# A two-layer block with a selective scan: later accumulating transfers, a later silu and router, spreads first, more convolution on TensorE

## The chip, the cores and the metric

One Trainium2 chip, of which the program uses one core. The metric is the device time of one execution in microseconds, the median of three runs.

## The reference

Two layers over `x` of 4 x 256 tokens with 512 features, all in float32. Only the second layer is touched by the change.

```python
xn = layernorm(x)
x = x + attention(xn) + ffn(xn)                 # layer 0
xn = layernorm(x)
x = x + ssm(xn) + moe(xn)                       # layer 1

def ssm(h):                                     # DIN = 1024, N = 16, K = 4
    x, z = split(h @ in_proj_w)                 # 512 -> 2 x 1024, then as b d l
    xc = silu(conv_b + sum(conv_w[:, k] * pad(x)[:, :, k:k + L] for k in range(4)))
    p = xc @ x_proj_w.T                         # 32 + 16 + 16 columns
    dt_r, Bm, Cm = rmsnorm of each part
    dt = softplus(dt_r @ dt_proj_w.T + dt_bias)
    h_t = exp(dt_t * A) * h_{t-1} + dt_t * B_t * xc_t        # 1024 x 16 states
    y_t = sum over n of h_t * C_t
    return ((y + D * xc) * silu(z)) @ out_proj_w.T

def moe(x):
    base = x @ base_W.T
    w = softmax(x @ router_W.T), top 2 of 8, normalised, 0 elsewhere
    mid = (x @ lora_A) * w                      # 8 experts x rank 16
    return base + 2 * (mid @ lora_B)
```

## The kernel before

The program is written by hand in order: every engine runs its instructions in the order in which the Python code emits them, and semaphores between the engines follow from the data. SyncE (SP) issues the plain transfers, GpSimd (POOL) the accumulating ones. VectorE is DVE, ScalarE ACT and TensorE PE.

Layer 0 and the preparation of batch 0 take the first 325 us. What the change touches is the scan phase after that. The four batches b are scanned one after the other, each as 32 units: eight chunks c of 128 channels times four groups g of four states (`PER` = 32 units in a batch, `NU` = 4 in a chunk). A unit holds 128 partitions (4 states x 32 channels) by 4 x 256 columns. Its steps are:

- `decays(u)`, ACT: four exponentials of 255 columns into one of four `decay` buffers, emitted three units ahead;
- `scan_in(u)`, DVE: `bx = B * (dt * xc)` (line 995). Before it stands a wait for the landed `du` of the chunk, the unit's decays, and the state sums of unit u-4, whose buffer `h` it is about to reuse;
- `scan(u)`: the scan on DVE (line 1009), then `h * C` on POOL (line 1014);
- `states_sum(u-1)`, PE: four matmuls that add the states into `ysum` (line 1026), with `D * xc` (line 1024) at a chunk's first unit. There is one `ysum`, so this first matmul waits until `take_sum` has copied the last chunk's sum to SBUF (ACT, line 1031);
- `gate`, POOL: `y * silu(z)` (line 1034).

`dt` and `dt * xc` come out as 128 channels by 256 columns; `send` stores a pair of chunks to memory (line 939) and `spread` reads one chunk back as 32 x 4 lines, in four transfers (line 944), into one of two buffers.

While a batch is scanned, the next one is prepared, and the outputs of earlier ones are finished. The pieces are hung on units by hand: `put(b, s, f, ...)` places a call ahead of the scan of unit s of batch b, `put_mid` between `scan_in` and `scan`, `put_late` after the scan and `put_end` after the sum. Within a unit, the copy of a finished sum (`take_sum`) and the decays come first. The pieces are:

- `norm_*`, then `px_mm` (line 763), the projection of a pair p of chunks of the next batch, two matmul groups in units 6 to 13;
- `conv_in` and `conv_taps`: the convolution over four taps. The first chunk of a pair goes over PE with diagonal weights (`dg`, made by ACT, line 810) from batch 1 on. The second one does so too for the pairs in `both`; else ACT makes three scaled copies (`tap`, line 791) and POOL adds them up (line 817);
- `conv_out`, `conv_silu` (ACT, line 826, with `gate_silu`, line 959, and a table load before and after), then `pp_mm`, `pp_square` and `pp_norm` (DVE, line 851);
- `step_in` and `step_exp` (ACT), `step_out` (POOL, lines 920, 922 and 924) and `step_x` (POOL, line 931): the next `dt` and `dt * xc`, with a `send` at the last of each;
- `pz_mm` and `gate_silu` for `silu(z)`;
- `router`, `route` (15 small DVE steps, lines 1061 to 1093), `expert_mid`, `expert_turn`, `expert_out`: the experts of two batches at a time;
- `dense` and `out_mm`: the base and the output projection, row block by row block. For batches 0 to 2 the scanned layer's output is not added on chip: `store_x` first writes the residual to the output, and `add_out` copies a PSUM group over `x` (ACT) and adds it to the output by an accumulating transfer (POOL). One such group holds `dense` and `expert_out`, the other `out_mm`.

PSUM has three general buffers (`psmm`), which all the groups above share.

Of the kernel before, what the change touches and what calls it, by code (L numbers as in the profile page):

```python
# [26 lines left out]
DC = DIN // P  # L27
# [14 lines left out]
def block_kernel(  # L42
# [25 lines left out]
    mm = nc.tensor.matmul  # L68
# [50 lines left out]
    live = {}  # L119
# [416 lines left out]
    first, second = latents(0), latents(1)  # L536
# [62 lines left out]
    first, second = latents(2), latents(3)  # L599
# [166 lines left out]

    both = ((1, 0), (1, 3), (2, 1), (2, 3), (3, 1), (3, 3))

# [345 lines left out]

    def dense(b, i, k):
        if k == 0:
            live["po", b, i] = psmm.tile([P, D], F32, tag="mm", name="po1")
        for hc in (2 * k, 2 * k + 1):
            mm(live["po", b, i], lhsT=xns[b][:, hc, i * P : (i + 1) * P], rhs=late_w["bw"][:, hc, :],
               start=(hc == 0), stop=False)  # L1120

    stored = {}

    def rows_of(tb):
        return out_d[tb * P : (tb + 1) * P, :]
# [3 lines left out]

    def add_out(tb, po):  # L1130

        nc.scalar.copy(x[:, tb, :], po)  # L1132
        d = nc.gpsimd.dma_start(rows_of(tb), x[:, tb, :], accum_op=ALU.add)
        tc.add_manual_dep(d.ins, stored[tb].ins.name, early, reason="sums in place")
        stored[tb] = d

    def expert_out(b, i):
        po, last = live["po", b, i], b == B - 1
        if last:
            mm(po, lhsT=ident, rhs=x[:, 2 * b + i, :], start=False, stop=False)  # L1140
        mm(po, lhsT=live["mt"][:, i * P : (i + 1) * P], rhs=late_w["lb"], start=False, stop=not last)
        if not last:
            add_out(2 * b + i, live.pop(("po", b, i)))

    def out_mm(b, i, c):
        if c == 0 and b < B - 1:
            live["po", b, i] = psmm.tile([P, D], F32, tag="mm", name="po2")
        mm(live["po", b, i], lhsT=xcs[b][:, c, i * P : (i + 1) * P], rhs=late_w["ow"][:, c, :],  # L1148
           start=(c == 0 and b < B - 1), stop=(c == DC - 1))
        if c == DC - 1 and b < B - 1:  # L1150
            add_out(2 * b + i, live.pop(("po", b, i)))

# [121 lines left out]

    at, mid_at, late_at, end_at = {}, {}, {}, {}
# [12 lines left out]
    def put_late(b, s, f, *a):  # L1288

        late_at.setdefault(b * PER + s, []).append((f, a))  # L1290

    for b in range(B):
        nxt = b + 1
        if b:
            put(b, 0, b_rows, b, 1)
            put(b, 0, spread, "du", b, 1)

            put(b, 0, gate_silu, b, 0, 1)
            for k, u in enumerate((0, 1, 1, 2)):
                put(b, u, dense, b - 1, k // 2, k % 2)  # L1300
            put(b, 2, expert_turn, b - 1)
            for i in range(2):
                put(b, 3, expert_out, b - 1, i)

            for (bo_, i), us in {
                1: {(0, 0): range(22, 30)},
# [3 lines left out]
            }[b].items():  # L1310
                for c, u in enumerate(us):
                    put(b, u, out_mm, bo_, i, c)
        else:
# [44 lines left out]
        if nxt < B:  # L1358
# [11 lines left out]
            for p in range(NP):  # L1370
                put(b, 2 * p if b else (5, 6, 9, 9)[p], load_x, nxt, p)
# [10 lines left out]
            put_late(b, 21, step_in, nxt, 0, 0)  # L1382
            put(b, 22, step_in, nxt, 0, 1)
            put(b, 22, c_rows, nxt, 0)
            put(b, 23, step_exp, nxt, 0, slice(0, 2))
            put(b, 23, step_exp, nxt, 0, slice(2, 4))
            put(b, 23, c_rows, nxt, 1)
            for q, us in enumerate(((24, 25, 26), (28, 30, 32))):
                for k in range(3):
                    put(b, us[k], step_out, nxt, 0, q, k)  # L1390
            put(b, 27, step_x, nxt, 0)
            put(b, 27, spread, "dt", nxt, 0)
            put(b, 29, spread, "du", nxt, 0)
            put(b, 33, step_x, nxt, 1)
            put(b, 30, b_rows, nxt, 0)
            put(b, 31, spread, "dt", nxt, 1)
            put(b, 23, load_z, nxt, 0)
# [3 lines left out]
            if b % 2 == 0:  # L1401
                for i, u in enumerate((16, 17, 19, 20)):
                    put(b, u, router, b, i)
                choice = route()
                for w, u in ((0, 22), (0, 23), (0, 24), (1, 25), (0, 25), (0, 26), (1, 27), (0, 27),
                             (0, 28), (1, 29), (0, 29), (1, 30), (0, 30), (0, 31), (0, 32)):
                    (put_mid if w else put_late)(b, u, next, choice)
                for i in range(2):
                    put_late(b, 32 + i, expert_mid, b, i)
# [15 lines left out]
    for u in range(total + 2):  # L1425
# [153 lines left out]
```

## Time and profile before

| | us |
|---|---|
| median of three runs | 832.85 (832.42 to 832.89) |
| the profiled execution | 835.05 |
| its span, first to last instruction | 833.0 |
| first `bx` of the scan phase | 325.5 |
| batch 0, 1, 2, 3 of the scan | 135.5, 122.9, 123.3, 125.8 |
| busy over the span: PE, DVE, ACT, POOL | 735.7, 652.1, 557.2, 509.0 |
| mean granted clock of TensorE | 0.953 |

The span is shorter than the execution's time; the rest lies around the first and the last instruction. A row of the timeline gives the start, the busy time, the engine, the line and the operation with output and inputs; in brackets at its end stand the idle time of the engine before it and what ended that. A wait for several semaphores is put down to the one that the profile shows as the last, which can be a neighbour of the right one where two end close together. The records of POOL are rough, above all for some units after a transfer was issued there, where neighbouring operations seem to overlap.

### The profile page before, as it was taken

Reading aid. Unit: us, or ns where it says so; the run is one execution under the profiler, and the core shown is the slowest. Engines: PE = TensorE matmul, PEld = TensorE weight load, DVE = VectorE, ACT = ScalarE, POOL = GpSimd, SP = SyncE. Lnnn points to the kernel's source line nnn. Section 1 sums busy time; section 2 is a strip of 40 time slices with the busy share of each in tenths; the row PEclk is TensorE's granted clock in tenths of the full one; section 3 lists DMA queues with packets and bytes.
Section 4 is the critical chain, followed back from the end, with each engine's and each line's share of the span. In section 5 each row is a group of like instructions: output and inputs, shape, how many; then the busy total and the mean of one; then the engine's idle time right before and its main releaser. Section 6 shows DMA issues by size and latency. Waiting matters only on the chain.

```text
span 833.0 us, 11255 instructions
## 1 busy us (share of the span) xinstructions
PE 735.7 (88%) x3834; PEld 428.6 (51%) x3834; DVE 652.1 (78%) x590; ACT 557.2 (67%) x1132; POOL 509.0 (61%) x406
## 2 busy tenths in 40 slices
PE   4999999999999999989887869788889878899985
PEld 2665545666555676656544346444346544334331
DVE  4586755287734435898699999899998899998996
ACT  4335574435556277599897798788898796865660
POOL 3223322001333333677969799969699978899875
PEclk9899999999999999979998979899999998999998
DMA  7234232001223332566395645534655534547500
GB/s 227 64 102 122 82 102 63 1 1 39 77 76 82 113 57 64 151 170 174 95 243 157 167 99 139 126 102 114 177 115 126 127 102 102 118 95 169 125 26 25
DMA packets 70371, 89.86 MB, mean 108 GB/s; under 512 B 12413, under 2 KB 52361, under 8 KB 70186
## 3 DMA queue, kind: packets, MB, share of 16 engines
q1 hardware_dynamic: 58794, 65.81, 29.8%
q0 software_dynamic: 10800, 21.50, 10.7%
q10 hardware_dynamic: 720, 1.84, 0.7%
q8 instruction: 30, 0.49, 0.3%
q14 instruction: 27, 0.22, 0.1%
HBM read 66.58 MB, written 13.37 MB: 96 GB/s over the span
## 4 chain that ended last, share of the span: by engine, by line
PE 49%; DVE 16%; POOL 11%; ACT 9%; issue 7%; DMA 7%; SPq 1%; POOLq 0%; ACTq 0%; DVEq 0%
PE pg L444 7%; POOL h L1014 6%; DVE h L1009 6%; PE pu L444 5%; DVE bx L995 4%; DMA dus<-dud 4%; PE px L763 4%; PE av L397 4%; PE po L469 3%; PE ysum L1026 3%; PE px L810 3%; PE pz L953 3%; PE scT L386 2%; DVE mpl L354 2%; ACT decay L983 2%
## 5 line engine op out<-in xcount | busy, mean ns | idle before, releaser
L1014 POOL TENSOR_TENSOR h<-h,cr 128x1024 f32<-128x1024 f32 (+1 forms) x130 | 312.8, 2432 | 50.6 <-DVE h L1009 41.2
L1009 DVE TENSOR_TENSOR_SCAN h<-decay,bx 128x1024 f32<-128x1024 f32 (+1 forms) x129 | 288.1, 2236 | 6.5 <-PE po L469 1.9
L983 ACT ACTIVATE decay<-dts,aneg 128x255 f32<-128x255 f32 x504 | 212.1, 501 | 35.9 <-DVE h L1009 17.7
L995 DVE TENSOR_TENSOR bx<-brow,dus 128x1024 f32<-128x1024 f32 x128 | 157.6, 1231 | 27.6 <-PE ysum L1026 10.9
L1026 PE MATMUL ysum<-h,stack 128*32 128x256 f32 x1024 | 87.6, 417 | 35.8 <-POOL h L1014 35.5
L456 POOL TENSOR_TENSOR hlo<-g,hhi 128x512 fp32r<-128x512 f32 x28 | 35.8, 1280 | 114.0 <-ACT hhi L455 114.0
L354 DVE TENSOR_REDUCE mpl<-sc 128x4 f32<-128x1024 f32 x64 | 76.7, 1220 | 22.2 <-PE sc L352 20.8
L427 POOL DMA_DIRECT2D wgu<-in_wgu x56 | 31.0, 554 | 94.6 <-PE pg L444 93.6
L388 ACT ACTIVATE pe<-scT 128x1024 f32<-128x1024 f32 x64 | 64.0, 1023 | 22.9 <-PE sc L352 14.2
L1026 PEld LDWEIGHTS ysum<-h,stack 128*32 128x32 f32 x1024 | 21.8, 112 | 90.1 <-POOL h L1014 61.6
L1148 PE MATMUL po<-ow,xc 128*128 128x512 f32 x128 | 65.4, 634 | 2.9 <-ACT x L1132 2.5
L953 PE MATMUL pz<-xn1T,w_in 128*128 128x256 f32 x256 | 65.0, 400 | 0.0
L763 PE MATMUL px<-xn1T,w_in 128*128 128x256 f32 x256 | 63.5, 395 | 0.4 <-ACT sz L959 0.3
L953 PEld LDWEIGHTS pz<-xn1T,w_in 128*128 128x128 f32 x256 | 48.8, 197 | 18.9 <-issue 11.2
L763 PEld LDWEIGHTS px<-xn1T,w_in 128*128 128x128 f32 x256 | 49.2, 197 | 14.2 <-issue 4.9
L452 DVE SCALAR_TENSOR_TENSOR g<-g,pg 128x512 f32<-128x512 f32 x28 | 19.2, 687 | 43.0 <-ACT g L451 43.0
L444 PE MATMUL pg<-xhi,wgu 128*128 128x512 f32 x112 | 49.6, 443 | 1.4 <-ACT xhi L244 1.4
L469 PE MATMUL po<-wd,hhi 128*128 128x512 f32 x112 | 49.4, 441 | 0.0
L444 PE MATMUL pu<-xhi,wgu 128*128 128x512 f32 x112 | 47.4, 423 | 0.8 <-DVE g L454 0.8
L455 ACT CAST hhi<-g 128x512 fp32r<-128x512 f32 x28 | 17.3, 620 | 45.8 <-DVE g L454 45.8
L444 PE MATMUL pg<-xlo,wgu 128*128 128x512 f32 x112 | 45.3, 404 | 0.7 <-DVE xlo L251 0.7
L444 PE MATMUL pu<-xlo,wgu 128*128 128x512 f32 x112 | 44.3, 396 | 0.0
(239 smaller groups left out, 1296.8 us busy)
## 6 DMA issues: line engine op xcount, KB each, us to landing
dts<-dtd SPq DMA_DIRECT2D x124, 128.0 KB, 3.1
dus<-dud SPq DMA_DIRECT2D x124, 128.0 KB, 3.3
wgu<-in_wgu POOLq DMA_DIRECT2D x56, 256.0 KB, 2.8
w_in<-in_inz SPq DMA_DIRECT2D x16, 512.0 KB, 5.3
w_in<-in_inx SPq DMA_DIRECT2D x14, 512.0 KB, 5.3
dtd<-dt SPq DMA_DIRECT2D x15, 256.0 KB, 2.2
dud<-du SPq DMA_DIRECT2D x15, 256.0 KB, 2.2
wd<-in_wd POOLq DMA_DIRECT2D x7, 512.0 KB, 3.6
```

What stands on the lines that cost most here:

```text
L354: nc.vector.tensor_reduce(mpl2[b % 2][:, qb, 2 * hp : 2 * hp + 2, 16 + 2 * gq : 18 + 2 * gq], sc.rearrange("p i (f k) -> p i f k", f=2), A ...
L388: nc.scalar.activation(pes[b, k][:, 2 * t : 2 * t + 2, :], sc, AF.Exp)
L444: mm(ps, lhsT=wgus[i][:, hc, :], rhs=xs[j][:, hc, :], start=(hc == 0 and j == 0), stop=(hc == HC - 1 and j == 1))
L469: mm(po, lhsT=hids[th][j][:, m, i * P : (i + 1) * P], rhs=wd[:, m, :], start=False, stop=(m == MC - 1 and j == 1))
L763: mm(px[:, i, :], lhsT=w[:, i, hc, :], rhs=xns[b][:, hc, :], start=(hc == 0), stop=(hc == HC - 1))
L953: mm(pz[:, i, :], lhsT=w[:, i, hc, :], rhs=xns[b][:, hc, :], start=(hc == 0), stop=(hc == HC - 1))
L983: made["da", u] = nc.scalar.activation(da[:, k, 1:], live["dts", b, c][:, k, 1:], AF.Exp, scale=aneg[:, c, k, g : g + 1])
L995: nc.vector.tensor_tensor(bx, brow[g // 2][:, g % 2, :].unsqueeze(1).to_broadcast([P, NG, S]), live["dus", b, c], ALU.mult)
L1009: nc.vector.tensor_tensor_scan(h[:, n].rearrange("p n t -> p (n t)"), da[:, n].rearrange("p n t -> p (n t)"), bx[:, n].rearrange("p n t -> ...
L1014: made["hc", u] = (nc.vector if k == NG - 1 else nc.gpsimd).tensor_tensor(h[:, n], h[:, n], crows[b][:, g, :].unsqueeze(1).to_broadcast([P ...
L1026: made["sum", u] = mm(ysum[k * NB : (k + 1) * NB, :], lhsT=stack, rhs=hc[:, k, :], start=False, stop=(g == NU - 1))
L1148: mm(live["po", b, i], lhsT=xcs[b][:, c, i * P : (i + 1) * P], rhs=late_w["ow"][:, c, :], start=(c == 0 and b < B - 1), stop=(c == DC - 1))
```

## The change

It does the following.

- `both` takes in all pairs of batches 2 and 3, so four more chunks are convolved on PE.
- `dense` closes its own PSUM group, and the experts' matmul (`expert_out`) goes into the group of `out_mm`, ahead of its last matmul. `add_out` only copies; the accumulating transfer (`add_to`) is emitted at a given unit, two to 22 units later, after that unit's scan.
- `conv_out` of the last pair and `conv_silu` go from unit 16 to 17 in batches 1 and 2, where the sum's copy stands first (in batch 0 they are at 17 already). `pp_mm` goes from 17 (end) and 18 to 19 and 20, and what follows, up to the first `dt` and `du` of the next batch, goes one unit later.
- The router goes from units 16 to 20 to units 24 to 26, `route` from 22 to 28 on (so that it ends in unit 6 of the next batch), and `expert_mid` and `expert_turn` into later units.
- A new list, `first_at`, is emitted ahead of a unit's other pieces. In batches 1 to 3 all spreads are on it, and so are the first spreads of the next batch.
- `step_out`, one `step_x`, one `load_x` and the last `out_mm` groups are moved by one to three units.

```diff
-    both = ((1, 0), (1, 3), (2, 1), (2, 3), (3, 1), (3, 3))
+    both = ((1, 0), (1, 3)) + tuple((b, p) for b in (2, 3) for p in range(NP))
...
-    def dense(b, i, k):
+    def dense(b, i, k, u=None):
...
-               start=(hc == 0), stop=False)
+               start=(hc == 0), stop=(hc == HC - 1 and b < B - 1))
+        if k and b < B - 1:
+            add_out(2 * b + i, live.pop(("po", b, i)), u)
...
-    def add_out(tb, po):
+    def add_out(tb, po, u):
 
         nc.scalar.copy(x[:, tb, :], po)
+        late_at.setdefault(u, []).append((add_to, (tb,)))
+
+    def add_to(tb):
         d = nc.gpsimd.dma_start(rows_of(tb), x[:, tb, :], accum_op=ALU.add)
...
+        last = c == DC - 1
+        if last and b < B - 1:
+            expert_out(b, i)
         mm(live["po", b, i], lhsT=xcs[b][:, c, i * P : (i + 1) * P], rhs=late_w["ow"][:, c, :],
-           start=(c == 0 and b < B - 1), stop=(c == DC - 1))
-        if c == DC - 1 and b < B - 1:
-            add_out(2 * b + i, live.pop(("po", b, i)))
+           start=first, stop=last)
+        if last and b < B - 1:
+            add_out(2 * b + i, live.pop(("po", b, i)), u)
...
-            put(b, 0, spread, "du", b, 1)
+            put_first(b, 0, spread, "du", b, 1)
...
-                put(b, u, dense, b - 1, k // 2, k % 2)
-            put(b, 2, expert_turn, b - 1)
-            for i in range(2):
-                put(b, 3, expert_out, b - 1, i)
+                put(b, u, dense, b - 1, k // 2, k % 2, b * PER + (3, 15)[k // 2])
...
-                1: {(0, 0): range(22, 30)},
-                2: {(0, 1): (4, 4, 4, 5, 5, 5, 6, 7)},
-                3: {(1, 0): (4, 4, 4, 5, 5, 5, 6, 6), (1, 1): (6, 7, 7, 7, 8, 8, 8, 9),
-                    (2, 0): (9, 9, 10, 10, 10, 11, 11, 11), (2, 1): (12, 12, 12, 13, 13, 13, 14, 15)},
+                1: {(0, 0): (range(22, 30), PER + 19)},
+                2: {(0, 1): ((4, 4, 4, 5, 5, 5, 6, 7), 17)},
+                3: {(1, 0): ((4, 4, 4, 5, 5, 5, 6, 6), 17), (1, 1): ((6, 7, 7, 7, 8, 8, 8, 9), 19),
+                    (2, 0): ((11, 11, 12, 12, 12, 13, 13, 13), 20),
+                    (2, 1): ((14, 14, 14, 15, 15, 15, 16, 16), 21)},
...
+            if b == 1:
+                put_late(b, 19, expert_mid, 0, 0)
+                put_late(b, 20, expert_mid, 0, 1)
+                put(b, 21, expert_turn, 0)
+            if b == 3:
+                put(b, 3, expert_turn, 1)
+                put_late(b, 10, expert_mid, 2, 0)
+                put_late(b, 15, expert_mid, 2, 1)
+                put(b, 12, expert_turn, 2)
...
-        for q, us in enumerate(((5, 6, 7), (10, 12, 14)) if b else ((9, 10, 11), (13, 15, 16))):
+        for q, us in enumerate(((4, 5, 7), (9, 11, 12)) if b else ((9, 10, 11), (13, 15, 16))):
...
-        for p, u in ((2, 8 if b else 11), (3, 16 if b else 17)):
+        for p, u in ((2, 8 if b else 11), (3, 13 if b else 17)):
...
-            put(b, 3 if c == 2 and not b else 4 * c - 6 + o, spread, "dt", b, c)
-            put(b, 4 * c - 4 + o, spread, "du", b, c)
+            to = put_first if b else put
+            to(b, 3 if c == 2 and not b else 4 * c - 6 + o, spread, "dt", b, c)
+            to(b, 4 * c - 4 + o, spread, "du", b, c)
...
-            put(b, 16 + o, conv_out, nxt, NP - 1)
-            put(b, 16 + o, conv_silu, nxt, (b, 2))
-            put_end(b, 17, pp_mm, nxt, 0)
-            put(b, 18, pp_mm, nxt, 1)
-            put(b, 19, pp_square, nxt)
-            put_mid(b, 21, pp_norm, nxt)
+            put(b, 17, conv_out, nxt, NP - 1)
+            put(b, 17, conv_silu, nxt, (b, 2))
+            put(b, 19, pp_mm, nxt, 0)
+            put(b, 20, pp_mm, nxt, 1)
+            put(b, 21, pp_square, nxt)
+            put_mid(b, 22, pp_norm, nxt)
...
-                for i, u in enumerate((16, 17, 19, 20)):
+                for i, u in enumerate((24, 25, 25, 26)):
                     put(b, u, router, b, i)
...
-        for f, a in at.get(u, ()):
-            f(*a)
+        for d in (first_at, at):
+            for f, a in d.get(u, ()):
+                f(*a)
```

More of the change, by code (lines that the diff above doesn't have):

```diff
@@ L1137, in expert_out, with out_mm @@
     def expert_out(b, i):
-        po, last = live["po", b, i], b == B - 1
-        if last:
+        po = live["po", b, i]
+        if b == B - 1:
             mm(po, lhsT=ident, rhs=x[:, 2 * b + i, :], start=False, stop=False)
-        mm(po, lhsT=live["mt"][:, i * P : (i + 1) * P], rhs=late_w["lb"], start=False, stop=not last)
-        if not last:
-            add_out(2 * b + i, live.pop(("po", b, i)))
-    def out_mm(b, i, c):
-        if c == 0 and b < B - 1:
+        mm(po, lhsT=live["mt"][:, i * P : (i + 1) * P], rhs=late_w["lb"], start=False, stop=False)
+    def out_mm(b, i, c, u=None):
+        first = c == 0 and b < B - 1
+        if first:
             live["po", b, i] = psmm.tile([P, D], F32, tag="mm", name="po2")
+        last = c == DC - 1
+        if last and b < B - 1:
+            expert_out(b, i)
         mm(live["po", b, i], lhsT=xcs[b][:, c, i * P : (i + 1) * P], rhs=late_w["ow"][:, c, :],
-           start=(c == 0 and b < B - 1), stop=(c == DC - 1))
-        if c == DC - 1 and b < B - 1:
-            add_out(2 * b + i, live.pop(("po", b, i)))
+           start=first, stop=last)
+        if last and b < B - 1:
+            add_out(2 * b + i, live.pop(("po", b, i)), u)
     def out_x(b, i, side=0):
@@ L1272, in load_late @@
             late_w[n] = t
-    at, mid_at, late_at, end_at = {}, {}, {}, {}
+    first_at, at, mid_at, late_at, end_at = {}, {}, {}, {}, {}
     def put(b, s, f, *a):
@@ L1290, in put_late, with put_first @@
         late_at.setdefault(b * PER + s, []).append((f, a))
+    def put_first(b, s, f, *a):
+        first_at.setdefault(b * PER + s, []).append((f, a))
     for b in range(B):
@@ L1295, in block_kernel @@
             put(b, 0, b_rows, b, 1)
-            put(b, 0, spread, "du", b, 1)
+            put_first(b, 0, spread, "du", b, 1)
             put(b, 0, gate_silu, b, 0, 1)
             for k, u in enumerate((0, 1, 1, 2)):
-                put(b, u, dense, b - 1, k // 2, k % 2)
-            put(b, 2, expert_turn, b - 1)
-            for i in range(2):
-                put(b, 3, expert_out, b - 1, i)
-            for (bo_, i), us in {
-                1: {(0, 0): range(22, 30)},
[3 rows of a table removed]
+                put(b, u, dense, b - 1, k // 2, k % 2, b * PER + (3, 15)[k // 2])
+            for (bo_, i), (us, to) in {
+                1: {(0, 0): (range(22, 30), PER + 19)},
[4 rows of a table added]
             }[b].items():
                 for c, u in enumerate(us):
-                    put(b, u, out_mm, bo_, i, c)
+                    put(b, u, out_mm, bo_, i, c, b * PER + to)
+            if b == 1:
[7 more added lines that the diff above has]
+                put(b, 12, expert_turn, 2)
         else:
@@ L1370, in block_kernel @@
             for p in range(NP):
-                put(b, 2 * p if b else (5, 6, 9, 9)[p], load_x, nxt, p)
+                put(b, (0, 2, 4, 8)[p] if b else (5, 6, 9, 9)[p], load_x, nxt, p)
                 for i in range(2):
@@ L1375, in block_kernel @@
                 put(b, 9 + o + 2 * p, conv_taps, nxt, p)
-            put(b, 16 + o, conv_out, nxt, NP - 1)
-            put(b, 16 + o, conv_silu, nxt, (b, 2))
-            put_end(b, 17, pp_mm, nxt, 0)
-            put(b, 18, pp_mm, nxt, 1)
-            put(b, 19, pp_square, nxt)
-            put_mid(b, 21, pp_norm, nxt)
[L1382 to L1388, printed above, removed]
+            put(b, 17, conv_out, nxt, NP - 1)
[4 more added lines that the diff above has]
+            put_mid(b, 22, pp_norm, nxt)
+            put_late(b, 22, step_in, nxt, 0, 0)
+            put(b, 23, step_in, nxt, 0, 1)
+            put(b, 23, c_rows, nxt, 0)
+            put(b, 24, step_exp, nxt, 0, slice(0, 2))
+            put(b, 24, step_exp, nxt, 0, slice(2, 4))
+            put(b, 24, c_rows, nxt, 1)
+            for q, us in enumerate(((25, 26, 27), (29, 31, 32))):
                 for k in range(3):
                     put(b, us[k], step_out, nxt, 0, q, k)
-            put(b, 27, step_x, nxt, 0)
-            put(b, 27, spread, "dt", nxt, 0)
-            put(b, 29, spread, "du", nxt, 0)
+            put(b, 28, step_x, nxt, 0)
+            put_first(b, 28, spread, "dt", nxt, 0)
+            put_first(b, 30, spread, "du", nxt, 0)
             put(b, 33, step_x, nxt, 1)
             put(b, 30, b_rows, nxt, 0)
-            put(b, 31, spread, "dt", nxt, 1)
+            put_first(b, 31, spread, "dt", nxt, 1)
             put(b, 23, load_z, nxt, 0)
@@ L1401, in block_kernel @@
             if b % 2 == 0:
-                for i, u in enumerate((16, 17, 19, 20)):
+                for i, u in enumerate((24, 25, 25, 26)):
                     put(b, u, router, b, i)
                 choice = route()
[L1405 to L1409, printed above, removed]
+                for w, u in ((0, 0), (0, 1), (0, 2), (1, 3), (0, 3), (0, 4), (1, 5), (0, 5),
+                             (0, 6), (1, 7), (0, 7), (1, 8), (0, 8), (0, 9), (0, 10)):
+                    (put_mid if w else put_late)(b, 28 + u, next, choice)
         else:
-            put(b, 12, expert_turn, b)
+            put(b, 18, expert_turn, b)
             put(b, 17, dense, b, 0, 0)
             put(b, 18, dense, b, 0, 1)
-            put(b, 18, expert_out, b, 0)
+            put(b, 19, expert_out, b, 0)
             put(b, 20, dense, b, 1, 0)
```

## The prediction

> **What bounds the kernel now.** I read the windows view of the four batches first, then the waits of VectorE (DVE), then its timeline where it waits, then the engine that ends each wait. I write b.u for unit u of batch b.
>
> ```profile
> 325.50:461.00 135.50, 116.69 (x641) 76.25 (x640) 120.30 (x93) 113.46 (x258) 104.91 (x69) 0.92 0.62 160
> 461.00:583.90 122.90, 102.27 (x545) 57.61 (x544) 115.16 (x71) 104.56 (x236) 108.12 (x68) 0.92 0.49 127
> 583.90:707.20 123.30, 104.14 (x577) 61.09 (x575) 115.56 (x80) 102.44 (x235) 106.47 (x65) 0.94 0.51 126
> 707.20:833.00 125.80, 104.58 (x468) 42.30 (x468) 114.37 (x73) 72.09 (x155) 101.29 (x61) 0.96 0.39 93
> ```
>
> Busy times stand as PE, PEld, DVE, ACT, POOL. DVE leads in every batch. Its waits before `bx` (total, times, longest):
>
> ```profile
> DVE bx L995 <- PE ysum L1026: 10.9, 8, 2.3
> DVE bx L995 <- DMA dus<-dud: 9.1, 6, 3.5
> DVE bx L995 <- ACT decay L983: 4.5, 4, 1.7
> ```
>
> A unit is one `bx` (1.23 us) and one scan (2.29); undisturbed units start 3.59 us apart (508.23 minus 504.64), so 128 units need 459 of the scan's 507.5 us. The 48 left are the start (most of batch 0), the tail, DVE's own small operations, and waits of `bx`. Only the waits after unit 10 of each batch, and the small operations, are within this change's reach.
>
> ```profile
> 508.23 1.23 DVE L995 TENSOR_TENSOR bx<-brow,dus 128x1024 f32<-128x1024 f32 x1
> 512.76 1.23 DVE L995 TENSOR_TENSOR bx<-brow,dus 128x1024 f32<-128x1024 f32 x1 [0.98 <-ACT decay L983]
> ...
> 528.35 1.23 DVE L995 TENSOR_TENSOR bx<-brow,dus 128x1024 f32<-128x1024 f32 x1 [1.25 <-PE ysum L1026]
> ...
> 542.28 1.23 DVE L995 TENSOR_TENSOR bx<-brow,dus 128x1024 f32<-128x1024 f32 x1 [2.33 <-PE ysum L1026]
> 543.64 0.48 DVE L851 SCALAR_TENSOR_TENSOR nrm<-pp,lnw,rs 64x256 f32<-64x256 f32 x1
> ```
>
> This is batch 1. `bx` of unit u needs the sums of unit u-4. The wait at 512.76 is put down to ACT, but the sum of unit 1.10 ended at 512.56: PE again. From 1.13 (508.23) to 1.23 (549.93) DVE lost 5.8 us over ten undisturbed units; in batch 2 from 2.10 (620.03) to 2.23 (672.91) 6.2. Why the sums are late:
>
> ```profile
> 505.97 0.64 PE L1026 MATMUL ysum<-h,stack 128*32 128x256 f32 x8 [0.93 <-POOL h L1014]
> 506.54 2.00 PE L810 MATMUL px<-pad,dg 128*128 128x256 f32 x8
> 508.38 1.89 PE L810 MATMUL px<-pad,tap 128*128 128x256 f32 x8
> 510.10 1.89 PE L763 MATMUL px<-xn1T,w_in 128*128 128x256 f32 x8
> ...
> 533.90 1.22 PE L1024 MATMUL ysum<-xc,dgs 128*128 128x256 f32 x2 [5.32 <-ACT xc L1031]
> ```
>
> Up to 528 us PE is full: sums stand in its order behind projections and convolution. At 533.90 it has waited 5.32 us for ACT's copy of a finished sum, which stood behind `silu` and its two table loads:
>
> ```profile
> 528.48 1.28 ACT L826 ACT_TABLE_LOAD   x1
> 529.77 1.91 ACT L826 ACTIVATE xc<-xc 128x2048 f32<-128x2048 f32 x1
> 531.59 0.58 ACT L959 ACTIVATE sz<-pz 128x512 f32<-128x512 f32 x1
> 532.18 1.28 ACT L710 ACT_TABLE_LOAD   x1
> 533.48 0.37 ACT L1031 COPY xc<-ysum 128x256 f32<-128x256 f32 x1
> ```
>
> **The change, part by part.**
>
> *Silu behind the copy (batch 0: -1.3 us).* Batch 0's silu stays at unit 17, but its sums are no longer behind `pp_mm`, which goes from 17/18 to 19/20. 0.21 waited 1.32 us for the sum of 0.17, held up by `pp` until 418.9; now that sum can run at about 412. 0.20 keeps its 3.53 us: its `du` stands on SP behind a send that waits for POOL, and batch 0's orders of sends and spreads are the old ones. The router leaves PE there too (0.47 us at 0.19), but 0.20 waits for the same transfer, so I count nothing.
>
> *Spreads first (batch 3: -2.6 us).* In batch 3 the spread of `du` 3 at unit 8 is issued behind the send of pair 2:
>
> ```profile
> 744.99 0.38 SPq L939 DMA_DIRECT2D dud<-du  x1
> 745.46 2.77 SPq L944 DMA_DIRECT2D dus<-dud  x4
> ```
>
> It lands around 750-753 and `bx` at 752.92 waits 2.60. First in its unit, it waits only for the send of `dt` before it; with POOL's steps one unit earlier I get it landed some 10 us before 3.12. The same in 2.12 (1.03), 1.20 (0.86) and 2.20 (0.21); those are inside the sums of batches 1 and 2 below. Each spread moves four issues of 0.43 us past at most a send and a load on SP.
>
> *Convolution.* In batches 1 and 2 two further chunks each (for batches 2 and 3) go from POOL to PE: POOL loses 2 x 3 x 0.73 = 4.4 us a batch plus its waits for `tap`, PE gains 2 x 1.8 = 3.7 (506.54 to 510.10 for a pair), ACT is even (3.13 + 0.84 against 3.7 + 0.47).
>
> *Accumulating transfers.* POOL's waits for the `x` copies go (13.8 us in five waits, 4.45 in 1.5 and 5.01 in 2.5), but `step_out`, now at unit 4, meets ACT's four exponential steps in their place, with the `h` of 4 and so its sum queued behind it on POOL. Counting ACT in its new order (a dense copy of 0.55 each in 1 and 2, no `mt` copy, no wait of 1.22 and 0.81 for the one free PSUM buffer) they start at 478.2 instead of 480.0, so POOL has `e` at 481.7. Three steps of 1.28, four `h` of 2.36 and a gate of 0.73 later unit 1.7 is done at 495.7 instead of 497.8. PE's convolution of pair 0 can start at 496.3.
>
> *Batch 1 (-0.7 us).* PE from there, by the intervals of the timeline (pair of convolutions 3.56, projection 1.83 to 1.92, sum 0.57, `dgs` 0.53): the sum of 1.10 ends 15.0 later, 511.3, in time for 511.8, so the 0.94 goes. The sum of 1.12 ends at 520.2 where 1.16 is due at 519.0: 1.2 lost, a new wait. The sum of 1.14 ends at 528.6, 1.15 lost; 1.18 starts at 528.7, as before (528.35). From here PE is free, and the waits of 0.86 and 2.30 go. But the silu block is now later: sum of 1.15 at 529.2, copy 0.37, decay 1.65, two `xc` 0.84, loads and silus 5.05 give 537.1; three decays 4.89; then copy, decay, `mt` copy, square, PE, two roots (0.36, 1.65, 0.37, 0.38, 0.77, 0.90) give `rs` at 546.4. `nrm` sits behind the `bx` of 1.22 (543.05 + 1.23): it waits 2.1. 1.23 then starts at 549.2 against 549.93. The decay of 1.21 ends at 538.8 for 539.5, so it just passes.
>
> *Batch 2 (-1.5 us).* The same with its own numbers. The second `xn1T` copy ends at 609.4 (before 611.96), PE's convolution starts at 618.7, losses are 1.45 at 2.16, 1.15 at 2.18 and 1.75 at `nrm`; 2.23 starts at 671.4 against 672.91.
>
> *Router and route (+0.7, between 0 and +1.5).* Sixteen router matmuls and four copies move into units 24 to 26, where PE and ACT have room. The fifteen small DVE operations are as many as before. Four of them cost up to 1.3 us instead of 0.17, because POOL runs an operation of its own at that moment:
>
> ```profile
> 683.56 1.30 DVE L1069 TENSOR_TENSOR sel<-sel,m 128x32 f32<-128x32 f32 x1
> ...
> 683.55 1.26 POOL L922 TENSOR_TENSOR e<-e,lw 128x512 f32<-128x512 f32 x1
> ```
>
> Before, six of the late ones fall into units with a POOL step and cost 3.8 us in all over both routes. After, units 29, 31, 32, 33, 36 and 37 do: as many chances, but POOL may run later in four units in a row. Between nothing and 1.5 us more; I take 0.7.
>
> *Second copy of row block (2,1) (+0.5, between 0 and +0.9).* Each row block of `x` is copied and accumulated twice, as before; but the dense half of (2,1) is now sent at the end of unit 3.15, and the copy at 3.16 must wait until that transfer has read it. POOL can issue at 2.9 us into unit 16. By the row, these 256 KB transfers land 4.0 (479.95) to 6.7 us (755.23) after POOL's instruction starts; then come copy 0.55, the gate's silu 3.15, the sum's copy 0.37, the decay 1.65, so the decay of 3.20, queued behind them on ACT, ends at 12.6 to 15.3, where 14.36 is due. [...] At every other second copy ten units or more lie between. The experts' matmuls (0.95 us each) now stand in the output groups; units 3.14 and 3.15 then give PE 5.4 us each, 3.6 over, where a sum may be 7.8 late, so they cost nothing; without that cover it would be 3.6.
>
> Sum: -1.3 - 0.7 - 1.5 - 2.6 + 0.7 + 0.5 = -4.9 us. The profiled execution took 835.05 us (span 833.0, 2.05 around it), 2.2 above the median of 832.85; its 830.15 after the change stands for 828.0 at the median.
>
> **The rivals.** The common term is how late PE gets through the convolutions of batches 1 and 2. Every microsecond d by which it is later than worked out delays unit 18 and the `nrm` chain alike, and counts in both batches: -4.9 + 2d.
>
> Slower: the 3.7 us more on PE is not covered. It had only 1.3 us of idle time in the stretch (0.37 and 0.93), so the cover is the earlier start. If POOL isn't earlier (2.2) and ACT's copies and diagonals hold PE up 1.8 more, d = 4 and the time is 836. It becomes slower from d = 3.3. For it: PE is busy 38.28 of the 40 us from 489 on, POOL 39.69. Against: POOL loses 4.4 us there.
>
> No change: the wait for `e` eats the earlier start, d = 2.2 to 2.6: 832.4 to 833.1.
>
> More: `nrm`'s waits (2.1 and 1.75) don't arise, because ACT reaches the silu earlier than worked out: 824.
>
> **How the numbers follow.** The chance for the forecast is 0.45, for more 0.17, for no change 0.14, for slower 0.24. About 0.2% (1.7 us) is what a measurement here can tell. So faster 0.62, same 0.14, slower 0.24. The range reaches from the better case, 824, to the slower one, 836; the forecast's own is 825.5 to 830.5.
>
> **What would show it.** In the new profile: `bx` of 3.12 and 0.21 without waits; 2.60 and 1.32 gone; no POOL wait for ACT's `x` copy, but one of several us at `e` in unit 4; new waits of 1 to 1.5 us at 1.16 and 2.16; a wait of about 2 us of `nrm` on `rs`; L817 only 15 times. Wrong: waits at 16 and 18 of 3 us and more (slower rival), waits on ACT's decay at 1.21, 2.21 or 3.20, or a first spread that holds up sends behind it.

## The result, and the profile after

The change makes the kernel slower: 839.32 us (median of 18 runs, 834.38 to 844.83) against 833.63 (18 runs, 832.42 to 837.2) beside it, a ratio of 1.0068 with an interval of 1.0051 to 1.0086, so 4 to 7 us. Forecast were 828.0.

Each ratio in this text is taken against runs of the kernel before on the same chip, from the single runs without the disturbed ones, so it can differ by up to 0.2% from the quotient of the two medians. The profiled execution of the changed kernel took 844.83 us (span 842.8), 5.5 above its own median. Of that, 2.3 us lie ahead of the scan, where nothing was changed (first `bx` at 327.76 against 325.49). So the two traces are compared by batches and by waits. The windows view of the four batches, in the columns of the one before (stretch, length, busy PE, PEld, DVE, ACT, POOL, granted clock, DMA share, GB/s):

```profile
327.80:469.50 141.70, 121.77 (x643) 78.42 (x642) 118.87 (x83) 113.45 (x257) 104.91 (x69) 0.89 0.63 155
469.50:592.90 123.40, 103.58 (x539) 58.91 (x540) 115.41 (x81) 101.23 (x234) 102.98 (x62) 0.89 0.47 121
592.90:718.80 125.90, 111.73 (x609) 67.11 (x609) 114.08 (x71) 104.25 (x242) 103.00 (x60) 0.93 0.52 130
718.80:842.80 124.00, 106.94 (x470) 42.38 (x470) 115.46 (x82) 71.73 (x157) 101.33 (x62) 0.94 0.36 90
```

Batch 0 is 6.2 us longer (135.5 before), batch 1 0.5, batch 2 2.6 longer, batch 3 1.8 shorter. DVE's busy time is within 1.5 us of before in each; what grew is its waiting. DVE's waits (total, times, longest):

```profile
DVE nrm L851 <- ACT rs L715: 13.8, 4, 5.1
DVE bx L995 <- ACT decay L983: 9.4, 6, 3.1
DVE bx L995 <- PE ysum L1026: 7.2, 6, 2.3
DVE bx L995 <- DMA dus<-dud: 5.2, 2, 4.4
DVE bx L995 <- ACT pad L775: 3.4, 3, 1.4
```

Of what the change was reckoned to shorten, the waits for landings did shrink, 9.1 to 5.2. Those for sums stand at 7.2 where they were 10.9, but the 3.4 us put down to `pad` are waits for sums too: each of the three ends 0.25 us after the sum that it needs (at 528.68, a row shown below, that of 1.12, which ended at 528.43). So next to nothing is gained there. For decays `bx` waits 9.4 where it waited 4.5. All waits of `bx` together are 25.2 us against 24.5. What grew is `nrm`: 13.8 us where it waited 5.1 (one wait, ahead of the scan). The largest new wait, on DVE's timeline of batch 0:

```profile
424.51 1.23 DVE L995 TENSOR_TENSOR bx<-brow,dus 128x1024 f32<-128x1024 f32 x1
430.62 0.47 DVE L851 SCALAR_TENSOR_TENSOR nrm<-pp,lnw,rs 64x256 f32<-64x256 f32 x1 [4.88 <-ACT rs L715]
431.02 2.27 DVE L1009 TENSOR_TENSOR_SCAN h<-decay,bx 128x1024 f32<-128x1024 f32 x1
```

`nrm` stands in DVE's order between `bx` and the scan of unit 0.22, so the scan waits with it. ACT's timeline before that:

```profile
416.46 4.89 ACT L983 ACTIVATE decay<-dts,aneg 128x255 f32<-128x255 f32 x12
422.40 0.37 ACT L1031 COPY xc<-ysum 128x256 f32<-128x256 f32 x1 [1.05 <-PE ysum L1026]
426.50 1.70 ACT L983 ACTIVATE decay<-dts,aneg 128x255 f32<-128x255 f32 x4 [3.72 <-DMA dts<-dtd]
428.10 0.36 ACT L843 ACTIVATE sq<-pp 64x256 f32<-64x256 f32 x1
429.67 0.47 ACT L714 ACTIVATE rs<-pp,eps 64x256 f32<-64x256 f32 x1 [1.20 <-PE pp L844]
```

The four decays at 426.50 are those of unit 0.24, the first ones of chunk 6, emitted three units ahead, in unit 21. They wait 3.72 us for the landing of chunk 6's `dt`. Behind them in ACT's order now stands the square of the next batch's norm, moved from unit 19 to 21, and behind that PE, the roots and `nrm`. Before, the square ran at 418.39, ahead of these decays. The decays are needed three units later and can afford to wait; what was put behind them is needed at once.

PE was held up too, and its granted clock fell. PE's timeline there, and the windows around it (granted clock is the third number from the end):

```profile
428.52 1.11 PE L844 MATMUL pp<-sq,cst 64*64 64x256 f32 x2 [6.18 <-ACT sq L843]
429.56 1.22 PE L1024 MATMUL ysum<-xc,dgs 128*128 128x256 f32 x2
430.71 1.08 PE L1026 MATMUL ysum<-h,stack 128*32 128x256 f32 x8
...
435.59 0.64 PE L1026 MATMUL ysum<-h,stack 128*32 128x256 f32 x8
```

```profile
430.00:432.00 2.00, 2.00 (x11) 0.54 (x11) 1.38 (x2) 1.97 (x6) 0.00 (x0) 0.50 0.99 206
434.00:436.00 2.00, 2.00 (x15) 1.01 (x13) 1.97 (x2) 0.30 (x1) 2.00 (x2) 1.00 0.95 243
```

After 6.18 us without work the eight matmuls of a sum took 1.08 us; five microseconds later 0.64. The same comes back five units on, where PE waited 4.52 us and the router then ran at a granted clock of 0.50:

```profile
448.21 3.99 PE L1045 MATMUL pr<-rl,xn1T 128*128 128x136 f32 x16 [4.52 <-ACT cr L866]
451.99 1.06 PE L1024 MATMUL ysum<-xc,dgs 128*128 128x256 f32 x2
452.98 1.08 PE L1026 MATMUL ysum<-h,stack 128*32 128x256 f32 x8
```

The sum of 0.24 ended at 454.06 and `bx` of 0.28 followed at 454.32, 3.06 us late. The kernel before has such stretches as well, one of them in the same batch (granted clock 0.50 from 438 to 444 us), so they are not a cost of the change by themselves; what changed is which work falls into them:

```profile
439.48 1.22 PE L1024 MATMUL ysum<-xc,dgs 128*128 128x256 f32 x2 [5.52 <-ACT xc L1031]
```

In windows of 1 us the granted clock of the changed kernel falls from 1.00 to 0.50 some 4.4 and 3.5 us into the two waits (0.86 in 426 to 427, 0.60 in 447 to 448), and the slow stretches after them last 5 to 6 us. What sets either length was not shown.

Several lines came out as forecast: L817 is there 15 times, POOL no longer waits for `x` copies and waits up to 5.90 us at `e` in unit 4. `bx` of 1.16, 1.18 and 3.12 on DVE's timeline:

```profile
528.68 1.23 DVE L995 TENSOR_TENSOR bx<-brow,dus 128x1024 f32<-128x1024 f32 x1 [1.25 <-ACT pad L775]
...
537.07 1.23 DVE L995 TENSOR_TENSOR bx<-brow,dus 128x1024 f32<-128x1024 f32 x1 [1.25 <-PE ysum L1026]
...
762.65 1.23 DVE L995 TENSOR_TENSOR bx<-brow,dus 128x1024 f32<-128x1024 f32 x1
```

3.12 no longer waits (2.60 before). The wait of 1.25 at 1.16 is new, as forecast; that at 1.18 was there before.

From here on the loss of a unit is the time from its `bx` to the next `bx`, less 3.59 us. A wait ahead of the `bx` of 0.28 is thus a loss of 0.27. A unit that holds `nrm` without a wait loses 0.25 to 0.5 by it.

### The profile page after: what moved, and what is told of

Read it like the earlier page. It is cut to its first block, busy times and chain, and to the rows that moved or that the text cites. A ratio compares the mean times of both kernels' runs of the same rounds, so it can differ in the third digit from the quotient of the medians.

```text
span 842.8 us, 11311 instructions
## 1 busy us (share of the span) xinstructions
PE 753.8 (89%) x3866; PEld 438.8 (52%) x3866; DVE 650.5 (77%) x590; ACT 555.3 (66%) x1136; POOL 500.5 (59%) x394
## 4 chain that ended last, share of the span: by engine, by line
PE 55%; ACT 15%; DVE 12%; POOL 6%; issue 6%; DMA 4%; SPq 1%; ACTq 0%; POOLq 0%; DVEq 0%
PE pg L444 6%; PE px L763 6%; PE pu L444 5%; ACT decay L983 5%; POOL h L1014 4%; PE ysum L1026 4%; PE av L397 4%; DVE h L1009 3%; PE po L1155 3%; PE px L810 3%; DVE bx L995 3%; PE po L469 3%; PE pz L953 2%; PE scT L386 2%; DVE mpl L354 2%
## 5 line engine op out<-in xcount | busy, mean ns | idle before, releaser
L1014 POOL TENSOR_TENSOR h<-h,cr 128x1024 f32<-128x1024 f32 (+1 forms) x130 | 305.1, 2358 | 66.3 <-DVE h L1009 57.9
L1026 PE MATMUL ysum<-h,stack 128*32 128x256 f32 x1024 | 89.4, 423 | 14.2 <-POOL h L1014 14.1
L1155 PE MATMUL po<-ow,xc 128*128 128x512 f32 x128 | 70.5, 673 | 0.4 <-DVE xc L1464 0.4
L953 PE MATMUL pz<-xn1T,w_in 128*128 128x256 f32 x256 | 63.2, 392 | 0.0
```

The source lines that it names most:

```text
L953: mm(pz[:, i, :], lhsT=w[:, i, hc, :], rhs=xns[b][:, hc, :], start=(hc == 0), stop=(hc == HC - 1))
L1014: made["hc", u] = (nc.vector if k == NG - 1 else nc.gpsimd).tensor_tensor(h[:, n], h[:, n], crows[b][:, g, :].unsqueeze(1).to_broadcast([P ...
L1026: made["sum", u] = mm(ysum[k * NB : (k + 1) * NB, :], lhsT=stack, rhs=hc[:, k, :], start=False, stop=(g == NU - 1))
```

## The experiments

After the result there were three theories. A: the square, moved behind decays that wait for a landing, costs what is missing. B: the convolution on PE is not covered. C: the router, moved to units 24 to 26, meets a late PE and ACT.

**A, with the square of batch 0 alone.** The square of the norm made in batch 0 goes to unit 20, ahead of the decays of 0.24.

```diff
-            put(b, 21, pp_square, nxt)
+            put(b, 21 if b else 20, pp_square, nxt)
```

> The changed kernel with one piece moved: in batch 0 the square of the next batch's norm stands at unit 20 instead of 21, so ahead of the decays of unit 0.24 on ACT. Theory A (in batch 0 the square is queued behind the first decays of chunk 6, which wait for their dt to land; nrm then waits 4.9 us, and the lateness of ACT costs 3.1 us more at unit 27): nrm's wait in 0.22 falls from 4.9 to under 1 us, the kernel is 4 to 7 us faster than the changed one, so about 833 to 836 us. Theory B (the convolution on PE is the loss) and theory C (the router between units 24 and 26): no change beyond 1 us.

Measured: 832.2 us (827.95 to 836.85), ratio 0.9978 (0.9964 to 0.9993). One instruction, one unit earlier, is worth some 7 us by medians and by ratios. ACT's timeline:

```profile
413.39 4.89 ACT L983 ACTIVATE decay<-dts,aneg 128x255 f32<-128x255 f32 x12
418.68 0.38 ACT L843 ACTIVATE sq<-pp 64x256 f32<-64x256 f32 x1 [0.40 <-PE pp L837]
...
422.00 3.30 ACT L983 ACTIVATE decay<-dts,aneg 128x255 f32<-128x255 f32 x8 [1.04 <-DMA dts<-dtd]
```

The square stands ahead of the decays, which still wait for their landing, and nobody waits for them. The `nrm` of 0.22 does not wait. The loss of 3.06 at 0.27 fell to 1.24, and that of 1.13 at 2.06 went.

**The chain back to the old units.** `pp_mm` to `step_x` stand at the units of before, all else as in the changed kernel.

```diff
-            put(b, 19, pp_mm, nxt, 0)
-            put(b, 20, pp_mm, nxt, 1)
-            put(b, 21, pp_square, nxt)
+            put_end(b, 17, pp_mm, nxt, 0)
+            put(b, 18, pp_mm, nxt, 1)
+            put(b, 19, pp_square, nxt)
...
```

> The changed kernel with the whole chain from pp_mm to the first step_x of the next batch one to two units earlier, at the units of the kernel before (pp at 17 end and 18, square 19, nrm 21, step_in 21 and 22, step_exp 23, step_out from 24); silu stays at 17, spreads stay first. Theory A: the nrm wait of batch 0 and the waits at unit 27 of all three batches go (4.9 + 3.1 + 2.3 + 1.3), the sums of 0.17, 1.17 and 2.17 are again behind pp (1.3 to 2.3 each back): 5 to 8 us faster than the changed kernel, about 831 to 834 us. Theories B and C: within 2 us of the changed kernel.

Measured: 832.58 us, ratio 0.9975 (0.9945 to 1.0006). The loss of the changed kernel is gone here too, so it lies in this chain (the profiled execution was 10 us above the median, so no line of it is used). This alone does not tell the chain's old place from the square's.

**C, the router back.**

```diff
-                for i, u in enumerate((24, 25, 25, 26)):
+                for i, u in enumerate((16, 17, 19, 20)):
```

> The changed kernel with the router of batches 0 and 2 at units 16, 17, 19 and 20 again, all else (route, experts) as changed. Theory C (at units 24 to 26 the router's matmuls wait 4.5 us for a PSUM buffer and hold up the sums of 23 and 24): the waits at 0.27 (3.1 us) and 2.27 (1.3 us) go, 3 to 4.5 us faster than the changed kernel, about 835 to 836. Theory A: those waits stay for the most part, since ACT is late by itself; at most 1.5 us faster.

Measured: 840.29 us, ratio 1.0082 (1.0061 to 1.0103), no better than the changed kernel. The losses at 0.27 and 2.27 fell to 0.36 and 0, but 0.22, 1.22 and 2.22 lost 3.02, 2.96 and 4.66 us with `nrm` (5.22, 1.73 and 2.88 in the changed kernel). In 0.22 no decay waited for a landing here; two copies of the router's results, at 418.13 and 421.32, stood on ACT ahead of the square instead. So the router is not what makes the kernel slower. Its new place is not free either: in four of the five runs of the changed kernel that have batch 0's square at 20, PE waits 4.52 us ahead of the router again and 0.27 loses 1.2 to 1.6. The old place together with a mended square was not run.

**B, the old division of the convolution.**

```diff
-    both = ((1, 0), (1, 3)) + tuple((b, p) for b in (2, 3) for p in range(NP))
+    both = ((1, 0), (1, 3), (2, 1), (2, 3), (3, 1), (3, 3))
```

> The changed kernel with the convolution split of the kernel before (four chunks back on POOL). Theory B: the waits at units 16 and 18 of batches 1 and 2 (1.25 + 1.25 + 1.44 + 1.25 us) and part of nrm's waits go: 3 to 6 us faster than the changed kernel. Theory A: POOL's three extra operations delay the sums instead, and the time is within 1.5 us of the changed kernel.

Measured: 838.26 us, ratio 1.0039 (1.0020 to 1.0059). It gives back 1 us by the medians and 2.4 by the ratios. The losses at 1.15 and 2.15 (1.21 and 1.40) went, but 1.26 and 2.13 lost 2.44 and 2.41; 0.22 loses 5.26 us, as in the changed kernel. B is at most a part, not the cause.

**A again, in all batches.**

```diff
-            put(b, 21, pp_square, nxt)
+            put(b, 20, pp_square, nxt)
```

> The changed kernel with ScalarE's square of the next batch's norm at unit 20 in every batch, where the changed kernel has it at 21 and the run before this one moved it in batch 0 alone. Theory A (the square stands behind a pair of decays that waits for a landing, and the wait for nrm at unit 22 follows from it): the waits for nrm at 1.22 and 2.22 (1.38 and 2.53 us in the changed kernel, 1.78 and 1.61 with the square moved in batch 0 alone) fall below 1 us as well, 829 to 831 us, 1.5 to 3 us faster than with batch 0's square alone. Rival (in batches 1 and 2 the wait is the take_sum chain itself, not the square): both waits stay, and the time stays at 832.

Measured: 827.86 us (825.82 to 831.63), ratio 0.9946 (0.9924 to 0.9968). Between the changed kernel and this one lie 1.0068 minus 0.9946, 1.2% or 10 us: the whole loss and more. DVE's waits:

```profile
DVE bx L995 <- PE ysum L1026: 7.0, 4, 2.4
DVE bx L995 <- DMA dus<-dud: 5.8, 3, 5.2
DVE nrm L851 <- ACT rs L715: 5.1, 1, 5.1
...
DVE bx L995 <- ACT decay L983: 1.6, 3, 0.6
```

`nrm` is back at the 5.1 us that lie ahead of the scan, and the waits for decays fell from 9.4 to 1.6. In batches 1 and 2 the square had stood behind more of ACT's queue rather than behind a landing. In batch 1 of the changed kernel it stood behind a sum's copy, four decays and another copy,

```profile
549.86 0.35 ACT L1031 COPY xc<-ysum 128x256 f32<-128x256 f32 x1
550.11 1.71 ACT L983 ACTIVATE decay<-dts,aneg 128x255 f32<-128x255 f32 x4
551.72 0.36 ACT L1112 COPY mt<-pt 128x256 f32<-128x256 f32 x1
551.97 0.38 ACT L843 ACTIVATE sq<-pp 64x256 f32<-64x256 f32 x1
```

while at unit 20 it comes right behind the twelve decays ahead of that copy.

**A by its other end: the landing.** The square stays at 21; batch 0's spread of chunk 6's `dt` goes from unit 19 to the head of unit 18, ahead of the two loads of `bw` that stood before it.

```diff
+            if b == 0 and c == 6:
+                put_first(b, 18, spread, "dt", b, c)
+            else:
+                to(b, 3 if c == 2 and not b else 4 * c - 6 + o, spread, "dt", b, c)
-            to(b, 3 if c == 2 and not b else 4 * c - 6 + o, spread, "dt", b, c)
```

> The changed kernel with the square left at unit 21; batch 0's dt rows of chunk 6 are asked for one unit earlier, ahead of the two base-weight loads that stood before them in SyncE's order. Theory A (the decays of chunk 6 wait for that landing, and the square stands behind them): the rows land at 421 to 424 us where they landed at 426.4, ScalarE's square of the norm comes 3 to 5 us earlier, the wait for nrm at 0.22 falls from 4.9 to 0.5 to 2 us and the time by 3 to 7 us, to 832 to 836. Rival (the square is late for its matmuls, pp, whatever the landing): the wait at 0.22 stays above 4 us and the time at 838 to 840.

Measured: 835.78 us, ratio 1.0032 (1.0016 to 1.0049), 3 to 3.5 us faster than the changed kernel. SP's queue, first in the changed kernel, then here:

```profile
414.67 0.91 SPq L1277 DMA_DIRECT2D bw<-in_base  x2
415.68 2.42 SPq L944 DMA_DIRECT2D dts<-dtd  x4
```

```profile
411.89 1.79 SPq L944 DMA_DIRECT2D dts<-dtd  x4
413.73 3.86 SPq L1277 DMA_DIRECT2D bw<-in_base  x4
```

The rows of this spread, which had landed at 426.4, were there before 419.77, when the decays of 0.24 ran without a wait for them; the `nrm` of 0.22 waited 0.82 us,

```profile
423.42 0.47 DVE L851 SCALAR_TENSOR_TENSOR nrm<-pp,lnw,rs 64x256 f32<-64x256 f32 x1 [0.82 <-ACT rs L715]
```

while 1.22 and 2.22 kept losses of 3.07 and 2.54. So in batch 0 it was that landing, in this execution. The execution was a quick one, 831.77 us or 4 below its median, and the median gives back only half of what the square's move did; how late the rows land in the others isn't known.

**Spreads first, alone.** The kernel before, with `first_at` for its spreads and nothing else changed.

```diff
+            to = put_first if b else put
-            put(b, 4 * c - 4 + o, spread, "du", b, c)
+            to(b, 4 * c - 4 + o, spread, "du", b, c)
...
```

> The kernel before with one part of the change alone: the row-to-partition spreads of a unit are issued ahead of its other steps. The prediction's sum: the waits at 3.11 (2.56 us), 2.11 (1.03), 1.20 and 2.20 (about .9 and .2 of them) go and nothing new comes, 829 to 831 us, 2.5 to 4.5 us faster than before. Rival (the spread's place in a unit does not set its landing, the queue's earlier loads do): the waits stay, 832 to 834.

Measured: 832.64 us, ratio 1.0003 (0.9990 to 1.0017): nothing. 3.11 lost nothing any more (2.56 before), as forecast, but 2.13 lost 2.58 (1.56), 1.13 1.41 (0.94) and 2.19 0.89 (0.21).

**The kernel before once more.**

> The kernel before, unchanged, in a second profile. The prediction read single waits off one execution: 2.56 us at 3.11, 1.71 at 0.12, 1.03 at 2.11, 0.86 at 1.19. If they belong to the program, they stand here within 0.3 us of that. Rival (waits for a landing that are a draw of that execution): some of them are gone, 3.11's above all, and the span is 1 to 3 us below 833.0.

Measured: 833.84 us, span 831.8. The `bx` of 3.12 in this execution:

```profile
751.55 1.23 DVE L995 TENSOR_TENSOR bx<-brow,dus 128x1024 f32<-128x1024 f32 x1 [1.55 <-ACT decay L983]
```

1.55 us and ended by a decay, in place of 2.60 ended by a landing. At 0.12 it lost 0.61 in place of 1.71, at 2.06 0.94 in place of 0.15, at 2.20 1.09 in place of 2.07; 1.19 and 2.11 hardly moved. Between these two executions single waits differ by up to 1.1 us. The losses at 1.13 and 2.19 rose here too, without any change (to 1.38 and 1.03), so much of what stood against the spreads above may be such a draw.

**Spreads back, with the square mended.**

```diff
-            to = put_first if b else put
+            to = put
...
```

> The changed kernel with the square at unit 20 in all batches, and the spreads back in their old places among a unit's steps. If spreads first brings what the prediction counted (3.11, parts of 2.11, 1.19, 2.19), this is 2.5 to 4.5 us slower than the same kernel with spreads first: 830.5 to 832. Rival (their place in the unit is worth nothing, as in the kernel before with that part alone): 827 to 829.

Measured: 829.01 us, ratio 0.9938 (0.9914 to 0.9962), the same as with the spreads first. 3.11 loses nothing here either: another part of the change frees it as well (the transfers do so alone, below).

**Transfers right behind their copies.** The changed kernel with batch 0's square at 20, and each accumulating transfer issued with its copy.

```diff
-        late_at.setdefault(u, []).append((add_to, (tb,)))
+        add_to(tb)
```

> The changed kernel with batch 0's square at unit 20, and the accumulating transfers issued right behind their copies, as in the kernel before. If issuing them units behind brings what the prediction counted (GpSimd does not wait for ScalarE's copy): GpSimd waits .5 to 1.5 us at some of the 14 places and 0 to 3 us are lost against the same kernel with the transfers behind, 832 to 835. Rival (GpSimd has the time to wait in those units): no wait of the scan comes of it, and the time stays at 832.

Measured: 843.66 us, ratio 1.0137 (1.0113 to 1.0162), against 0.9978 with the transfers behind: 1.6%, 13 us. Neither side had that. POOL waits for the copies again (13.8 us in seven waits), and works off what has piled up behind them without a gap. Three units of the scan carry most of the loss, 1.03, 2.01 and 3.03, each by one small DVE operation; here they are, then POOL's timeline around the second:

```profile
474.67 3.74 DVE L1084 TENSOR_TENSOR sel<-sel,b 128x32 f32<-128x32 f32 x1
...
590.51 5.34 DVE L735 SCALAR_TENSOR_TENSOR sh<-mv,rsn 128x2 f32<-128x2 f32 x1
...
726.66 4.07 DVE L1084 TENSOR_TENSOR sel<-sel,b 128x32 f32<-128x32 f32 x1
```

```profile
588.75 2.61 POOL L1014 TENSOR_TENSOR h<-h,cr 128x1024 f32<-128x1024 f32 x1
591.08 1.50 POOL L931 TENSOR_TENSOR du<-dt,xc 128x512 f32<-128x512 f32 x1
592.29 1.13 POOL L1138 DMA_DIRECT2D out<-x  x1
592.90 2.93 POOL L1014 TENSOR_TENSOR h<-h,cr 128x1024 f32<-128x1024 f32 x1
597.24 0.89 POOL L1138 DMA_DIRECT2D out<-x  x1 [1.41 <-ACT x L1134]
```

Operations of 0.15 and 0.17 us in other places took 13.2 us together, about the whole loss. That of 590.51 ended at 595.85; POOL's unbroken run had ended at 595.83. That of 474.67 ended at 478.41, and POOL's run there at 478.36. The third ended at 730.73.

**Transfers behind, alone.** The kernel before, where only the transfers go: experts' halves to units 8 to 10 (they were in 5), the other groups 4 to 7 units behind their copies.

```diff
         nc.scalar.copy(x[:, tb, :], po)
+        late_at.setdefault(send_at.pop(0), []).append((add_to, (tb,)))
+
+    def add_to(tb):
         d = nc.gpsimd.dma_start(rows_of(tb), x[:, tb, :], accum_op=ALU.add)
```

> The kernel before with one part alone: each accumulating transfer is issued some units behind ScalarE's copy (experts' halves at units 8 and 9 or 10 in place of right behind the copies in unit 5, products 4 to 7 units behind). If that part carries the 4.5 us that the changed kernel with the square at 20 gains: GpSimd's waits for the copies (13.8 us in five waits) go, h*C comes earlier behind them, the waits at 1.13 and 2.13 shrink by 1 us and more each, 829 to 831 us. Rival (it gives room that only the moved chain can use): 832 to 834.

Measured: 829.53 us (826.72 to 831.63), ratio 0.9950 (0.9929 to 0.9971). This one part carries as much as the whole change with its square mended. POOL's waits, of the kernel before and of this one:

```profile
POOL out L1133 <- ACT x L1132: 13.8, 5, 5.0
```

```profile
POOL e L920 <- ACT e L892: 8.6, 7, 2.5
```

The 13.8 us for copies are gone; the waits at `e` grew from 2.9 to 8.6. What DVE had lost at 1.13 (0.94), 2.11 (1.03), 2.13 (1.56) and 3.11 (2.56) became zero. That these had followed from POOL's late `h * C`, `dt` and `du` fits, but was not followed wait by wait.

**The chain alone, and with the transfers.** The kernel before with the chain at the changed kernel's units and the square at 20; then the same with the transfers behind.

```diff
-            put_end(b, 17, pp_mm, nxt, 0)
-            put(b, 18, pp_mm, nxt, 1)
-            put(b, 19, pp_square, nxt)
+            put(b, 19, pp_mm, nxt, 0)
+            put(b, 20, pp_mm, nxt, 1)
+            put(b, 20, pp_square, nxt)
...
```

> The kernel before with one part alone: the chain of the next batch's norm (silu, pp, norm, step) later as in the changed kernel, but with the square at unit 20. Theory A (the chain's move is worth its forecast once the square stands ahead of the decays): the waits at units 20 and 21 (1.28 and .48; 2.30 and .48; 2.07 and .48) go, no nrm wait above .5 comes, 828 to 830. Rival (the chain's move pays only with the convolution and the transfers moved as well): 832 to 834.

Measured: 835.23 us, ratio 1.0010 (0.9987 to 1.0034). The losses at 0.20, 1.20 and 2.20 (1.28, 2.30, 2.07) went or fell to 0.5, but 1.26 lost 2.60, 2.22 1.96 and 2.01 3.37, the last by L735, which took 3.57 us there, to 595.54.

> The kernel before with two parts: the transfers issued behind their copies, and the chain moved with its square at unit 20. Theory (the chain's move frees the waits at 19 to 21, 5.8 and 2.8 us in the profile of batches 1 and 2, and the transfers behind take away what stood against it: the wait of 3.38 at 2.01, GpSimd back to back): 827.5 to 830. Rival (the gain needs the convolution and the router moved too): 832 to 835, as with the chain alone.

Measured: 829.67 us, ratio 0.9945 (0.9923 to 0.9968), the same as with the transfers alone. The 3.37 at 2.01 went, but the chain's own gain was given back, mostly at 1.28 (1.12) and 2.22 (1.71). So the chain's move is worth nothing measurable here, and with the square at 21, in the changed kernel, it costs 10 us.

**The best of them.** The changed kernel with the square at 20 and the old `both`.

> The changed kernel with the square at unit 20 in all batches and the old division of the convolution between TensorE and GpSimd. The waits of 1.23 and 1.41 at 1.15 and 2.15 go (TensorE has 3.7 us less in those stretches); GpSimd has 4.4 us more. Theory B's remainder: 826 to 827.5, faster than both kernels. Rival (GpSimd's lateness costs as much, waits of 1.5 to 2.5 us at 2.13 and 1.17): 828 to 829.

Measured: 825.44 us (824.53 to 826.94), ratio 0.9899 (0.9874 to 0.9924): faster than both kernels. Against the same with more convolution on PE (0.9946, on another occasion) that is 2 to 4 us, by medians and by ratios. From the first `bx` to the end the profiles show 1.8 of them: the losses at 1.15 and 2.15 (1.22 and 1.41) went, and 0.27 took 1.23 back.

## Why the prediction was wrong

- *Silu behind the copy, batch 0: -1.3.* This is the step that failed. The wait that it named went, 1.28 at 0.20. But it followed the move of `pp` only as far as PE's sums. For batches 1 and 2 the prediction worked ACT's queue through to `nrm`; for batch 0 it put that wait at nothing, without a reason. The square moved with `pp`, past the decays of chunk 6, whose rows come over SP behind a load of `w_in` and two of `bw`; the prediction did not ask when they land. In place of -1.3 stand +4.88 at `nrm`, then 3.06 at 0.27, where the router's matmuls ran at a granted clock of 0.50; with the square at 20 in all batches, batch 0 took 133.29 us in place of 141.77.
- *Batches 1 and 2: -0.7 and -1.5.* They came as +0.5 and +2.6. `nrm`'s waits were forecast at 2.1 and 1.75 and came as 1.38 and 2.53; the waits at 16 and 18 as 1.2 to 1.4, as worked out. What was missed is units 27 and 28, 2.2 us in batch 1, and in batch 2 the losses at 2.11 and 2.13, which were to go and stayed at 0.70 and 1.56. The forecast took both `nrm` waits for unavoidable. Moving one instruction past a sum's copy, a few decays and another copy removed them: the working took the order on ACT as given.
- *Spreads first: -2.6.* Nothing in the time, by both runs that test it. The 2.60 was one execution's wait for one landing, 1.55 in the next. In the profiles spreads first did take it away, but the transfers alone did so too, so it could not be counted on top of them.
- *Router and route: +0.7.* The router's old place gained nothing. The 30 small DVE operations took 8.2 us after against 9.1, so in that execution the sign was wrong and the size small. "PE and ACT have room" in 24 to 26 was wrong for this kernel. With the square mended in all batches the loss at 0.27 and 2.27 went in one run, but was 1.26 and 1.95 in another and 1.23 and 0 in the best one.
- *Convolution and accumulating transfers.* The forecast let both meet in one number, "POOL 2.1 us earlier". Apart, the transfers are worth -4.5 us, nearly the whole predicted sum, and the convolution costs 2 to 4. The rival "slower", with 836 us, named the nearest time, but for another reason: its sign, waits of 3 us and more at 16 and 18, did not come, and the uncovered convolution is not what made the kernel slower.
- *Second copy of (2,1): +0.5.* No run shows the 0.5, the middle of its two bounds. In the profile the transfer of the dense half, issued on POOL at 780.00, landed 5.1 us later; 3.19 lost 0.11 and 3.20 nothing: about zero, inside the bounds.

The sum of -4.9 agrees with the kernel with its square mended (-4.5), but its terms do not; that agreement is no proof of them. Not settled is how the rest divides. Beyond the transfers alone, the best kernel gains another 0.5%, from router, experts in the output groups and moved steps together with the chain and the spreads, which alone gained nothing; the first three were not run apart.

## What to carry to other kernels

When a chain is moved in an engine's order, look at each of its instructions for what now stands ahead of it and waits: a wait that costs nothing where it is becomes the price of what is put behind it (here 3.72 us for a landing, and behind them 4.88 us at `nrm`). A transfer issued right behind the copy that it reads held up here all that POOL had behind it (13.8 us of waits in the kernel before); with the transfers some units later those waits were gone and the time was 4.5 us lower. A wait read from one execution can be a draw, here by up to 1.1 us; before a sum rests on it, read it in a second one.

## What had not been expected of the hardware

- Small DVE operations of 0.15 to 0.17 us took 3.74, 5.34 and 4.07 us in the run with the transfers right behind their copies, and one took 3.57 us with the chain alone. The prediction had bounded them at 1.3 us, from rows in which one ended with a single POOL operation (at 684.86, POOL's at 684.81). The first two ended with the last of three POOL operations, to within 0.05 us (478.41 and 478.36, 595.85 and 595.83). So they did not wait for one operation; that they waited for a gap on POOL fits, but was not shown. In the kernel before, POOL's next operation had begun 0.09 us ahead of the end at 684.86:

```profile
684.77 2.36 POOL L1014 TENSOR_TENSOR h<-h,cr 128x1024 f32<-128x1024 f32 x1
```

- After waits of 6.18 and 4.52 us, PE ran at a granted clock of 0.50 for 5 to 6 us (0.64 us became 1.08 for a sum). So these waits of PE were paid for twice. The kernel before showed it too: in the prediction's own row at 533.90 two matmuls took 1.22 us after a wait of 5.32, at a granted clock of 0.50, where it reckons with 0.53.
